# A four-layer graph network on one core: a one-hot matrix in bf16, and three elementwise steps moved from VectorE to ScalarE

## The chip, the cores and the metric

The kernel runs on one core of one Trainium2 chip. The metric is the device time of one launch in microseconds (us). Three launches of the kernel before took 5717.65, 5735.95 and 5736.4 us; the median is 5735.95 us. One more execution, taken with the profiler, took 5731.62 us.

## The reference, cut to what matters

There are 64 graphs of 256 nodes with 128 features, and an adjacency matrix of zeros and ones for each. Four layers follow each other, each with a residual and a layer norm:

```python
# layer 0: the largest relu(p_i + q_j + b) over the neighbours j of i
h = relu(p[:, :, None, :] + q[:, None, :, :] + b) * adj[..., None];  x = LN(x + max(h, axis=2))
# layer 1: three ELU projections, two of them aggregated over the graph
in_rep, out_rep, node_rep = elu(x @ W_in.T + b_in), elu(x @ W_out.T + b_out), elu(x @ W_node.T + b_node)
upd = concat([adj @ in_rep, node_rep, adj.T @ out_rep]);             x = LN(x + tanh(upd @ W_upd.T + b_upd))
# layer 2: two normalised graph convolutions;                        x = LN(x + ...)
# layer 3: for each pair gelu(LN(m_j + m_i + b1)), summed over the neighbours, then a projection and a layer norm
agg = einsum('bijo,bij->bio', gelu(LN(m_j[:, None] + m_i[:, :, None] + b1)), adj); x = LN(x + LN(concat([x, agg]) @ W2 + b2))
```

## The kernel before, in words

For each half h of the neighbours (128 of them), the kernel lays the edges of a graph out in "slots": slot s holds the s-th neighbour of each node that has one. The nodes are sorted by their number of neighbours in that half, so that slot s only needs its first w columns (`RECTS`, 4800 columns in all, `WIDTH`). A matrix of ones and zeros, `hot`, then turns "feature of the s-th neighbour" into a matrix product: layer 0 is a product of `q3` with `hot` and a running maximum (line 665 and the following ones), layer 3 a product of `c3` with `hot`, a normalisation over the features, a Gelu and a running sum.

The sorting is a permutation for each half. `first` (lines 502 to 710) makes it so:

- L509: `nz`, the adjacency in bf16, made on VectorE by comparing `an` (fp32, just loaded) with 1. L511 makes `diff`, which is zero where an entry is 0 or 1.
- L516 and L519: `nz` is transposed by TensorE, and ScalarE copies the result to `aT`.
- L528 to L551: TensorE counts neighbours, ScalarE compares the counts of all nodes (`sign`), which gives each node its place.
- L556 to L561: `perm`, 128 x (2 x 2 x 256), the one-hot of the place, made by four comparisons of `iota_k` (0 to 255 in fp32) with `place`. It is stored in fp32; `as_bf16` reads the upper halves of its words as bf16, with a stride of two.
- L566 and L577: TensorE sorts the columns of `nz` with `perm_b` and transposes `perm_b`; ScalarE copies the results to `nzp` (L571) and `permT` (L581), then makes `rank` (L587) and `lack` (L591), which tells for each slot and node how many neighbours are missing.
- L615: `full`, one where `lack` is zero, on VectorE. SyncE stores it to DRAM (`fulls`, L620), from where layer 3 reads it back in small pieces (`fu`, L763).
- L629 to L641: `hot`, 24 comparisons of `rank` and two more.

`second` is layer 1 (`layer_1`, L215 on). Its node part is the product at L230, the bias at L233 (`nd`, on VectorE), and an ELU: an exponential on ScalarE (L194) and two VectorE instructions (L200, L201). `third` is layer 2 (`layer_2`, L261 on) and the start of layer 3: L810 multiplies `dn` by `perm` in fp32, and four of the ten column tiles of layer 3 (`TODO`, five for each half) are begun (`sums_of`, L718). `last` does the rest of layer 3 (L821 on): a multiplication by the inverse deviation (L839, which waits for its transfer `rs_s`), the Gelu (L841) and the sums (L492).

The program is unrolled over all 64 graphs. In each iteration the four stages run for four different graphs, and `together` mixes their steps by weights (34, 34, 14, 44). What the engines execute is not in this order: a planner at compile time puts an instruction as early as its operands and its buffer allow, where an engine would stand idle by its account. The trace shows it: `nz` is made some 34 us before its first reader, and the three small instructions at L787, L267 and L269 run right after their one buffer comes free, most of an iteration ahead of their use. Each engine works through its own list, and waits at whatever is not ready.

Pools matter in a few places: `work` and `pair` have one buffer of each name (`nz`, `full`, `nd`, `elu_e`), `perm` has three, `permT` four.

Of the kernel before, what the change touches and what calls it, by code (L numbers as in the profile page):

```python
# [9 lines left out]
F32 = mybir.dt.float32  # L10
BF16 = mybir.dt.bfloat16
AF = mybir.ActivationFunctionType
ALU = mybir.AluOpType
# [6 lines left out]
P = 128  # L20
# [23 lines left out]
def kernel(  # L44
# [9 lines left out]
    nc = tc.nc  # L54
    B, N, D = x.shape
    assert N == 2 * P and D == P
    H = N // P
# [8 lines left out]
    nc.vector.memset(half, 0.5)  # L66
    eps_t = consts.tile([P, 1], F32, name="eps_t")
    nc.vector.memset(eps_t, EPS)
    minus1 = consts.tile([P, 1], F32, name="minus1")
    nc.vector.memset(minus1, -1.0)  # L70

# [85 lines left out]
    class Shared:  # L157
# [57 lines left out]
        def layer_1(self, s, an, aT, x1):  # L215

            work, psum, elu = self.work, self.psum, self.elu
            xT = self.to_features(x1, "xT_1", 1)
            yield
            io = work.tile([P, H, 2 * P], F32, name="io")  # L220
            pr = psum()
            for h in range(H):
                nc.tensor.matmul(pr[:, h * N:(h + 1) * N], xT[:, h * P:(h + 1) * P], w1_ioT, start=True, stop=True)
            yield
            for h in range(H):
                nc.vector.tensor_add(io[:, h], pr[:, h * N:(h + 1) * N], b1_io)
            yield from elu(io, io)
            yield
            pn = psum()
            nc.tensor.matmul(pn[:, :N], w1_nodeT, xT, start=True, stop=True)  # L230
            yield
            nd = work.tile([P, N], F32, name="nd")
            nc.vector.tensor_scalar(nd, pn[:, :N], b1_node, None, ALU.add)  # L233
            yield from elu(nd, nd)
            yield
            pg = psum()
            for h in range(H):
                nc.tensor.matmul(pg[:, :N], io[:, h, :P], aT[:, h], start=h == 0, stop=h == H - 1)
            for h in range(H):
                nc.tensor.matmul(pg[:, N:], io[:, h, P:], an[:, h], start=h == 0, stop=h == H - 1)  # L240
            yield
            ag = work.tile([P, 2, N], F32, name="ag")
            nc.scalar.copy(ag, pg.rearrange("p (c n) -> p c n", c=2))
            yield
            pu = psum()
            for h in range(H):
                cols = slice(h * P, (h + 1) * P)
                for c, part in enumerate((ag[:, 0], nd, ag[:, 1])):
                    nc.tensor.matmul(pu[:, cols], part[:, cols], w1_updT[:, c], start=c == 0, stop=c == 2)
            yield  # L250
            y = work.tile([P, H, P], F32, name="y", bufs=2)
            for h in range(H):
                nc.vector.tensor_add(y[:, h], pu[:, h * P:(h + 1) * P], b1_upd)
            nc.scalar.activation(y, y, AF.Tanh)
            yield
            nc.vector.tensor_add(y, y, x1)
            x2 = self.node_tile("x2")
            yield from self.layernorm(x2, y)
            s["x2"] = x2
# [94 lines left out]
    def sparse(ctx):  # L354
# [12 lines left out]
        nc.vector.tensor_copy(ident_b, ident)  # L367
        upto = cs.tile([P, P], BF16, name="upto")
        iota_k = cs.tile([P, N], F32, name="iota_k")
        down = cs.tile([1, N], BF16, name="down")  # L370
        slot1 = cs.tile([P, SLOTS], BF16, name="slot1")
        part1 = cs.tile([P, 1], F32, name="part1")
# [17 lines left out]
        with tc.tile_pool(name="cs_prep", bufs=1) as pp:  # L390
            t = pp.tile([P, P], F32, name="upto_f")
            nc.gpsimd.affine_select(
                out=t, in_=ones, compare_op=ALU.is_ge, fill=0.0, base=0, pattern=[[1, P]], channel_multiplier=-1
            )
            nc.vector.scalar_tensor_tensor(upto, ident, -FAR, t, ALU.mult, ALU.add)
            t = pp.tile([P, N], I32, name="iota_i")
            nc.gpsimd.iota(t, pattern=[[1, N]], base=0, channel_multiplier=0)
            nc.vector.tensor_copy(iota_k, t)
            t = pp.tile([P, 1], I32, name="part_i")
            nc.gpsimd.iota(t, pattern=[[0, 1]], base=0, channel_multiplier=1)  # L400
            part = pp.tile([P, 1], F32, name="part")
            nc.vector.tensor_copy(part, t)
            nc.vector.tensor_scalar(part1, part, 2.0, None, ALU.subtract)
            nc.vector.memset(part1[:3], float(SLOTS))
            nc.vector.tensor_scalar(down, iota_k[:1], -1.0, float(N - 1), ALU.mult, ALU.add)
            nc.vector.tensor_scalar(slot1, iota_k[:, :SLOTS], 1.0 - FAR, None, ALU.add)
            for h in range(H):
                for c in range(H):
                    nc.vector.tensor_scalar(
                        down_c[:, h, c:c + 1], part, -1.0, float(N - 1 - h * P), ALU.mult, ALU.add  # L410
                    )
            for t, slots in ((most, [w for s0, n, w in RECTS for _ in range(n)]), (least, SURE)):
                row = pp.tile([P, N], F32, name="slots")
                nc.vector.memset(row, 0.0)
                for w in slots:
                    if w:
                        nc.vector.tensor_scalar(row[:, :w], row[:, :w], 1.0, None, ALU.add)
                if t is most:
                    nc.vector.tensor_scalar(cover, row[:3], float(SLOTS), None, ALU.subtract)
                for hk in range(H):  # L420
                    pt = ps_mm.tile([P, 512], F32, name="mm")
                    nc.tensor.transpose(pt[:, :P], row[:, hk * P:(hk + 1) * P], ident)
                    for h in range(H):
                        nc.vector.tensor_copy(t[:, h, hk:hk + 1], pt[:, :1])
            t = pp.tile([P, 1], F32, name="gbe")
            nc.scalar.activation(t, be3, AF.Gelu)
            t3 = pp.tile([P, 3], F32, name="gbe3")
            nc.vector.tensor_copy(t3, t.broadcast_to([P, 3]))
            pt = ps_mm.tile([P, 512], F32, name="mm")
            nc.tensor.matmul(pt[:3, :P], t3, w3u[:, 1], start=True, stop=True)  # L430
            rest = pp.tile([3, P], F32, name="u_rest")
            nc.vector.tensor_copy(rest, pt[:3, :P])
            total = pp.tile([3, P], F32, name="u_total")
            nc.vector.memset(total, 0.0)
            for i in range(3):
                t = pp.tile([3, P], BF16, name="u_part")
                nc.vector.tensor_copy(t, rest)
                nc.vector.tensor_sub(rest, rest, t)
                nc.vector.scalar_tensor_tensor(total, t, ident[:3, i:i + 1], total, ALU.mult, ALU.add)
            nc.vector.tensor_scalar(ube, total, -1.0, None, ALU.mult)  # L440
            nc.vector.tensor_scalar(pick, ident[:ROWS, :ROWS], -BIG, None, ALU.mult)
            t = pp.tile([ROWS, g_n, g_w], F32, name="tail_f")
            nc.vector.memset(t, 1.0)
            nc.gpsimd.affine_select(
                out=t, in_=t, compare_op=ALU.is_equal, fill=0.0, base=-row_of(g_s0),
                pattern=[[-1, g_n], [0, g_w]], channel_multiplier=1,
            )
            nc.vector.tensor_copy(tail, t)
            nc.vector.memset(tail[:1, g_n - 1], 1.0)
# [23 lines left out]
        def as_bf16(t):  # L473

            return t.bitcast(BF16).rearrange("... (n two) -> ... n two", two=2)[..., 1]
# [26 lines left out]
        def first(g, s):  # L502
# [3 lines left out]
            an = state.tile([P, H, N], F32, name="an")  # L506
            nc.sync.dma_start(an, adj[ds(g, 1)].rearrange("b (h p) j -> p (b h) j", p=P))
            nz = pair.tile([P, H, N], BF16, name="nz")
            nc.vector.tensor_scalar(nz, an, 1.0, None, ALU.is_equal)  # L509
            diff = pair.tile([P, H, N], BF16, name="diff")  # L510
            nc.vector.scalar_tensor_tensor(diff, an, -1.0, an, ALU.add, ALU.mult)  # L511
            aT = state.tile([P, H, N], F32, name="aT", bufs=3)
# [41 lines left out]
            yield  # L554
            pos = work.tile([P, H, H], F32, name="place")
            nc.vector.tensor_scalar(pos, more, 0.5, 0.5 * (N - 1), ALU.mult, ALU.add)  # L556
            perm = state.tile([P, H, H, N], F32, name="perm", bufs=3)
            for h in range(H):
                for hi in range(H):
                    nc.vector.tensor_scalar(perm[:, h, hi], iota_k, pos[:, h, hi:hi + 1], None, ALU.is_equal)  # L560
            perm_b = as_bf16(perm)  # L561
            yield
            pz = psum()
            for h in range(H):
# [47 lines left out]
            s.update(an=an, aT=aT, perm=perm, permT=permT, lack=lack)  # L612

            full = pair.tile([ROWS, H, N], BF16, name="full")
            nc.vector.tensor_scalar(full, lack, 0.0, None, ALU.is_equal)  # L615
            s["fulls"] = fulls = dram.tile([H, WIDTH], BF16, name="fulls", bufs=5)
            for s0, n, w in RECTS:
                for a, m in ([(s0, n)] if s0 != g_s0 else [(s0, n - 1), (SLOTS - 1, 1)]):
# [163 lines left out]
        def third(g, s):  # L782
# [5 lines left out]

            yield from sh.layer_2(s, s["aT"], deg_of)
            yield  # L790
            x3, perm = s["x3"], s["perm"]

            x3T = sh.to_features(x3, "x3T")
            yield
# [348 lines left out]
```

## Time and profile before

| what | value |
|---|---|
| median of three runs | 5735.95 us (5717.65 to 5736.4) |
| profiled execution: time, span | 5731.62 us, 5729.7 us |
| TensorE matmul (PE) busy | 4529.9 us, 79% |
| VectorE (DVE) busy | 4834.4 us, 84%, 14654 instructions |
| ScalarE (ACT) busy | 4275.2 us, 75%, 6485 instructions |
| of that, loads of activation tables | 1236 x 1283 ns, 1585.8 us |
| the chain that ended last | PE 52%, DVE 29%, ACT 11%, issue 4%, DMA 3% |
| `perm` (L560) | 256 x 347 ns on DVE |
| `nz` (L509), `full` (L615), `nd` (L233) | 64 each, 421, 278 and 476 ns on DVE |

The span is that of all instructions; the time has the launch around it. A busy share is an average over all stages. The "chain that ended last" follows the work back from the last instruction, at each step to what released it, so its shares say which engine's work stood in the way, not how busy an engine was. "Idle before" in a group is the time in which the engine did nothing just ahead of such an instruction, with what ended it.

### The profile page before, as it was taken

To read this page: it belongs to the slowest core of one execution; us is meant where nothing else is said; L and a number is where in the kernel's file an instruction comes from. 1 tells how busy PE (TensorE), PEld (TensorE's weight loads), DVE (VectorE), ACT (ScalarE), POOL (GpSimd) and SP (SyncE) were. 2 spreads that over 40 slices of the span, in tenths; PEclk is the share of its full clock that TensorE was granted. 3 is DMA by queue.
4 is the path that set the end of the run, shared out by engine and by line. 5 is a ranking of instruction groups with operands and counts; after the bars stand their busy time and mean duration, and the time that the engine had idled before them with its cause. 6 is when DMAs were issued, how large, how long until landed. Compare 5 with 4: busy or idle time off the path is not lost.

```text
span 5729.7 us, 83531 instructions
## 1 busy us (share of the span) xinstructions
PE 4529.9 (79%) x27408; PEld 2508.7 (44%) x27408; DVE 4834.4 (84%) x14654; ACT 4275.2 (75%) x6485; POOL 1.9 (0%) x10
## 2 busy tenths in 40 slices
PE   5878878878778778788788788787887887877875
PEld 2444444444444444444444444444444444444443
DVE  6788888888888888888888888888888888888876
ACT  2577777777777777777777777777777777777785
POOL 0000000000000000000000000000000000000000
PEclk8888889889889889888898898898888887888986
DMA  0122222222212221221221222122212212221222
GB/s 22 44 70 63 62 63 72 62 63 66 69 57 70 65 63 63 72 63 62 63 72 62 63 65 70 59 68 65 63 62 72 64 62 63 69 66 60 68 65 74
DMA packets 292813, 365.15 MB, mean 64 GB/s; under 512 B 151952, under 2 KB 210448, under 8 KB 292368
## 3 DMA queue, kind: packets, MB, share of 16 engines
q1 hardware_dynamic: 292368, 359.73, 20.0%
q8 instruction: 217, 3.56, 0.3%
q14 instruction: 228, 1.87, 0.1%
HBM read 345.07 MB, written 14.53 MB: 63 GB/s over the span
## 4 chain that ended last, share of the span: by engine, by line
PE 52%; DVE 29%; ACT 11%; issue 4%; DMA 3%; SPq 0%; DVEq 0%; POOL 0%; ACTq 0%
PE bigp L665 11%; PE bigp L728 8%; DVE pre L839 6%; PE mm L860 5%; DVE lanes L492 4%; PE mm L743 4%; DVE hot L629 4%; DVE pre L732 4%; DVE sums L492 3%; PE bigp L681 3%; DMA rs_s<-scale_line 2%; PE mm L870 2%; PE mm L296 2%; PE mm L699 2%; PE mm L647 2%
## 5 line engine op out<-in xcount | busy, mean ns | idle before, releaser
L665 PE MATMUL bigp<-hot,q 128*128 128x512 fp8e4 (+1 forms) x3840 | 1052.3, 371 | 66.6 <-DVE lanes L492 52.6
L728 PE MATMUL bigp<-hot,c 128*128 128x512 fp8e4 (+1 forms) x3840 | 928.8, 372 | 140.2 <-DVE pre L732 140.2
L732 DVE TENSOR_TENSOR pre<-bigp,dT 128x512 f32<-128x512 f32 (+6 forms) x1664 | 846.3, 530 | 37.8 <-PE bigp L728 33.5
L492 DVE TENSOR_TENSOR lanes<-bigp,lanes 128x512 f32<-128x512 f32 (+6 forms) x1536 | 772.7, 503 | 94.6 <-PE bigp L681 86.9
L839 DVE TENSOR_TENSOR pre<-pre,rs_s 128x1024 f32<-128x1024 f32 (+1 forms) x640 | 732.9, 1150 | 48.6 <-DMA rs_s<-scale_line 48.0
L736 ACT ACTIVATE sq<-pre 128x1024 f32<-128x1024 f32 (+1 forms) x640 | 638.5, 998 | 169.9 <-DVE pre L732 163.9
L841 ACT ACT_TABLE_LOAD x535 | 686.4, 1283 | 9.5
L492 DVE TENSOR_TENSOR sums<-pre,sums 128x1024 f32<-128x1024 f32 (+6 forms) x1024 | 628.8, 614 | 41.2 <-ACT pre L841 40.7
L745 ACT ACTIVATE row<-mm,eps_t 128x256 f32<-128x256 f32 (+1 forms) x640 | 289.6, 453 | 476.9 <-PE mm L743 476.7
L841 ACT ACTIVATE pre<-pre,be,g 128x1024 f32<-128x1024 f32 (+1 forms) x512 | 594.2, 1172 | 57.8 <-DVE pre L839 53.0
L743 PE MATMUL mm<-sq,ones 128*32 128x256 f32 (+1 forms) x5120 | 482.9, 440 | 135.2 <-ACT sq L736 135.2
L74 ACT ACT_TABLE_LOAD x445 | 570.9, 1283 | 7.5
L728 PEld LDWEIGHTS <-c 128*128 128x128 bf16 x3840 | 331.2, 98 | 550.5 <-issue 136.1
L665 PEld LDWEIGHTS <-q 128*128 128x128 bf16 x3840 | 310.8, 97 | 392.6 <-issue 112.0
L296 PE MATMUL mm<-aT,hs 128*128 128x256 f32 x512 | 232.3, 600 | 316.1 <-DVE hs L293 214.8
L629 DVE TENSOR_SCALAR hot<-rank 128x512 fp8e4<-128x512 bf16 (+5 forms) x1536 | 440.5, 348 | 0.0
L681 PEld LDWEIGHTS <-pick 42*128 42x128 bf16 x2944 | 155.8, 95 | 481.5 <-issue 474.2
L296 PEld LDWEIGHTS mm<-aT,hs 128*128 128x128 f32 x512 | 135.6, 293 | 425.8 <-issue 316.1
L860 PE MATMUL mm<-w3u,sums 128*128 128x128 f32 x2048 | 296.7, 289 | 18.4 <-DVE sums L492 16.1
L194 ACT ACT_TABLE_LOAD x221 | 283.5, 1283 | 3.9
L681 PE MATMUL bigp<-lack,pick 42*128 42x36 bf16 (+16 forms) x2944 | 285.7, 187 | 0.0
L860 PEld LDWEIGHTS mm<-w3u,sums 128*128 128x128 f32 x2048 | 254.5, 195 | 37.3 <-issue 17.6
(226 smaller groups left out, 7132.6 us busy)
## 6 DMA issues: line engine op xcount, KB each, us to landing
rs_s<-scale_line SPq DMA_DIRECT2D x512, 512.0 KB
rs_s<-scale_line SPq DMA_DIRECT2D x128, 352.0 KB
an<-in_adj SPq DMA_DIRECT2D x64, 256.0 KB
x<-in_x SPq DMA_DIRECT2D x64, 128.0 KB
line<-row SPq DMA_DIRECT2D x512, 4.0 KB
out<-o SPq DMA_DIRECT2D x64, 128.0 KB
fu<-fulls SPq DMA_DIRECT2D x192, 4.0 KB
vr<-line SPq DMA_DIRECT2D x192, 8.0 KB
```

The lines of the kernel that those rows point to most:

```text
L74: nc.scalar.activation(t, t, AF.Sqrt)
L492: nc.vector.tensor_tensor(lanes[:, :k, :w], src[:, i:i + k], lanes[:, :k, :w], op)
L629: nc.vector.tensor_scalar(hot[:, :, at:at + w], rank[:, :, :w], s0 + i + 1.0 - FAR, None, ALU.is_equal, saturate=False)
L665: nc.tensor.matmul(pt[:, :tl], q3[:, i, h], hot[:, h, t0:t0 + tl], start=i == 0, stop=False)
L681: nc.tensor.matmul(o_, l_, r_, start=False, stop=i == len(todo) - 1)
L728: nc.tensor.matmul(pt[:, :bl], c3[:, k, h], hot[:, h, t0 + b:t0 + b + bl], start=k == 0, stop=k == 2)
L732: nc.vector.tensor_add(block(pre[:, b:], n, w, at), block(pt, n, w, at), widen(dT[:, h, :w], n))
L736: nc.scalar.activation(sq[:, :tl], pre[:, :tl], AF.Square)
L743: nc.tensor.matmul(pr[q * Q:(q + 1) * Q, :tl // 4], ones[:, :Q], v4[:, :, q], start=True, stop=True)
L839: nc.vector.tensor_mul(pre[:, :tl], pre[:, :tl], rs[:, :tl])
L841: nc.scalar.activation(msg[:, :tl], pre[:, :tl], AF.Gelu, bias=be3, scale=g3)
L860: nc.tensor.matmul(pt[:, cols], lanes[:, k, cols], w3u[:, 1], start=k == 0, stop=False)
```

## The change

Four edits:

1. `perm` is bf16 and is compared with a bf16 copy of the iota, `iota_b` (made once). It is read directly as `perm_b`. Since the product at L810 wants fp32, `third` first copies it to an fp32 tile `perm_f` on ScalarE, 128 x 1024, in the pool with one buffer.
2. `nz` is a copy on ScalarE instead of a comparison on VectorE.
3. `full` is relu(1 - lack) on ScalarE instead of a comparison on VectorE. `lack` is a whole number of zero or more, so both give one at zero and zero elsewhere.
4. The bias of `nd` is added on ScalarE, which then also does its exponential.

```diff
+    one_t = consts.tile([P, 1], F32, name="one_t")
+    nc.vector.memset(one_t, 1.0)
...
             nd = work.tile([P, N], F32, name="nd")
-            nc.vector.tensor_scalar(nd, pn[:, :N], b1_node, None, ALU.add)
+            nc.scalar.activation(nd, pn[:, :N], AF.Identity, bias=b1_node)
             yield from elu(nd, nd)
...
+        iota_b = cs.tile([P, N], BF16, name="iota_b")
...
+            nc.vector.tensor_copy(iota_b, t)
...
             nz = pair.tile([P, H, N], BF16, name="nz")
-            nc.vector.tensor_scalar(nz, an, 1.0, None, ALU.is_equal)
+            nc.scalar.copy(nz, an)
...
-            perm = state.tile([P, H, H, N], F32, name="perm", bufs=3)
+            perm = state.tile([P, H, H, N], BF16, name="perm", bufs=3)
             for h in range(H):
                 for hi in range(H):
-                    nc.vector.tensor_scalar(perm[:, h, hi], iota_k, pos[:, h, hi:hi + 1], None, ALU.is_equal)
-            perm_b = as_bf16(perm)
+                    nc.vector.tensor_scalar(perm[:, h, hi], iota_b, pos[:, h, hi:hi + 1], None, ALU.is_equal)
+            perm_b = perm
...
             full = pair.tile([ROWS, H, N], BF16, name="full")
-            nc.vector.tensor_scalar(full, lack, 0.0, None, ALU.is_equal)
+            nc.scalar.activation(full, lack, AF.Relu, bias=one_t[:ROWS], scale=-1.0)
...
-            x3, perm = s["x3"], s["perm"]
+            x3 = s["x3"]
+            perm = work.tile([P, H, H, N], F32, name="perm_f")
+            nc.scalar.copy(perm, s["perm"])
```

## The prediction

> **What bounds the kernel now.** I read the page first. Its engine line and its chain line:
>
> ```profile
> PE 4529.9 (79%) x27408; PEld 2508.7 (44%) x27408; DVE 4834.4 (84%) x14654; ACT 4275.2 (75%) x6485; POOL 1.9 (0%) x10
> PE 52%; DVE 29%; ACT 11%; issue 4%; DMA 3%; SPq 0%; DVEq 0%; POOL 0%; ACTq 0%
> ```
>
> No engine is full, and the chain passes through three of them. So the change, which takes from the busiest (DVE) and gives to the least busy (ACT), must be read stage by stage. The timeline repeats itself every two graphs, 174 us. Busy times of one graph's 87 us, cut where its character changes (graph 24, whose one-hot is made at 2052 us), with the third stretch of its neighbour, graph 25; columns are PE, weight loads, DVE, ACT, POOL, granted clock:
>
> ```profile
> 2000.00:2043.00 43.00, 39.20 (x255) 22.28 (x255) 39.27 (x121) 31.00 (x45) 0.00 (x0) 0.96 0.20 63
> 2043.00:2052.30 9.30, 3.86 (x31) 2.27 (x28) 6.41 (x16) 8.04 (x20) 0.00 (x0) 1.00 0.33 114
> 2052.30:2069.50 17.20, 10.67 (x57) 5.91 (x58) 15.29 (x55) 16.45 (x23) 0.00 (x0) 0.70 0.02 4
> 2069.50:2087.00 17.50, 17.50 (x102) 8.73 (x101) 12.98 (x37) 12.00 (x17) 0.00 (x0) 0.91 0.40 127
> ...
> 2138.80:2158.00 19.20, 10.14 (x57) 5.16 (x58) 16.25 (x56) 16.84 (x23) 0.00 (x0) 0.68 0.09 24
> ```
>
> Stretch 1 belongs to PE and DVE (91% each), stretch 4 to PE (100%). In stretch 3, ACT works 16.45 of 17.2 us while PE waits; with graph 25 it works 16.84 of 19.2. The four edited steps in the groups of instructions (busy us, mean ns, idle before), with rows that price them:
>
> ```profile
> L560 DVE TENSOR_SCALAR perm<-iota_k,place 128x256 f32<-128x256 f32 x256 | 72.7, 347 | 0.1
> L233 DVE TENSOR_SCALAR nd<-mm,b_node 128x256 f32<-128x256 f32 x64 | 30.5, 476 | 5.7 <-PE mm L230 5.6
> L509 DVE TENSOR_SCALAR nz<-an 128x512 bf16<-128x512 f32 x64 | 26.9, 421 | 4.0 <-DMA an<-in_adj 3.6 <-PE mm L566 0.5
> L615 DVE TENSOR_SCALAR full<-lack 42x512 bf16<-42x512 bf16 x64 | 17.8, 278 | 0.0
> L591 ACT ACTIVATE lack<-mm,part 42x512 bf16<-42x512 f32 x64 | 44.2, 691 | 0.0
> L745 ACT ACTIVATE row<-mm,eps_t 128x256 f32<-128x256 f32 x512 | 238.1, 465 | 339.0 <-PE mm L743 338.7
> L736 ACT ACTIVATE sq<-pre 128x1024 f32<-128x1024 f32 x512 | 538.7, 1052 | 167.2 <-DVE pre L732 163.9 <-DVE total_m L688 3.1 <-DVE hs L308 0.2
> ```
>
> Last the ACT timeline of graph 24 around `lack` and around the exponential of `hs` (start, duration):
>
> ```profile
> 2055.50 0.69 ACT L591 ACTIVATE lack<-mm,part 42x512 bf16<-42x512 f32 x1
> 2056.21 1.28 ACT L194 ACT_TABLE_LOAD   x1
> ...
> 2064.87 0.42 ACT L194 ACTIVATE elu_e<-hs 128x256 f32<-128x256 f32 x1
> 2065.31 1.28 ACT L74 ACT_TABLE_LOAD   x1
> 2066.60 0.22 ACT L74 ACTIVATE vr<-vr 108x16 f32<-108x16 f32 x1
> ```
>
> ACT runs without a gap from 2053.6 to 2069. DVE's L200 on that `hs` starts at 2065.78, 0.49 us after the exponential; DVE's L75 on that `vr` at 2066.99, 0.17 us after the root. L75 stands between the two halves of L293, and PE's L296 at 2067.49 waits for those.
>
> [...] L509 (fp32 in) takes 421 ns for 512 elements, L615 (bf16 to bf16) 278, a difference of 143[...]. [...] of 1236 loads none stands at a copy, at L591 or L745. So the change needs no load of its own.
>
> **The change part by part, for one graph.**
>
> *Off DVE.* `nz` 0.42, `full` 0.28, `nd` 0.48, and the four `perm` instructions [...] 347 becomes 280. Together 1.44 us, 92 us over 64 graphs. It is not the gain:
> - `nz` runs at 2008 us. The chain in order of time passes through it for none of the 64 graphs: DVE waits for PE (0.27 us at 2012.1) soon after. I take -0.1; bounds 0 and -0.42.
> - `perm`: PE waits for it 245.5 us in 64 times, but what is late next is ACT. Graph 24: `nzp` (L571) starts at 2053.61 as a Gelu ends, so an earlier L566 gives nothing. Graph 25: ACT waits 0.19 us for L566, so 0.19 is the most.
> - `full` and `nd` stand in a DVE run that the chain follows in half the graphs, but the ACT lag below replaces it.
>
> *On PE*: nothing. The transposes L577 read `perm` with a stride of two and take 217 ns at their shortest, L516 on the contiguous `nz` 219.
>
> *On ACT*[...] the rows above: `nz` 128x512 0.61 (the Abs of `diff`, same size, 0.63), `full` 42x512 with bias 0.69, `nd` 128x256 with bias 0.46, `perm_f` 128x1024 1.05. Less 0.09 overlap each, 2.45 us a graph, 157 us in all: 75% becomes 77%. No DMA is added; SyncE's stores of `full` follow it, and are read back a stage later.
>
> Where they land:
> - `full` becomes ready as `lack` ends. Graph 24: no gap, everything behind is 0.60 later, the exponential of `io` first (2.2 us of slack before DVE wants it), then `row`, `sq`, `agg`, a Gelu, `hs`, `vr`. Graph 25: ACT idles 0.46 after `lack` and gains 0.19 from `perm`, so 0 to 0.05.
> - `nd` in graph 24: L230 ends at 2062.6, a microsecond before the table load for `hs`, so it goes ahead: +0.37. In graph 25 L230 ends at 2154.2, after that load began, and ACT idles 0.46 ahead of the exponential of `nd`: nothing.
> - So in graph 24 `hs` and `vr` come 0.97 later. L75 has 0.17 of slack, so L293 and L296 come 0.80 later (DVE's own relief of about 0.9 is void, since it waits), and stretch 4, where PE is full, begins so much later. With `full` alone it is 0.43. Bounds 0 (both placed behind `vr`) and 0.97.
> - `nz` and `perm_f` (1.47) can go as soon as their buffers are free, after L566 and L810 of the graph before; L810 ends at 2004 us. The small instructions of L787 to L269 do the same, an iteration ahead. That is stretch 1, where ACT idles 12 of 43 us, 3.3 at 2025. Cover is thin in one place: DVE takes the sums at 2009.52, straight after a Gelu ending at 2009.36; a copy ahead of that costs up to 1.05. Bounds 0 and 1.47; I take 0.3, a fifth.
>
> *Sum*: mean of 0.80 and 0.05 is 0.43; +0.30 - 0.10 = 0.63 us a graph. Times 62 (two graphs pass while the pipeline fills): 39 us on the profiled execution's 5731.6, hence 5771. Its median stood 4.3 higher: **5775**, +0.7%.
>
> **Rivals.**
>
> *All hidden.* The planner puts `full` and `nd` into gaps[...] and DVE's relief pays for what is left. For it: 25% of ACT is idle. Against it: not where `lack` is. 5740 (5722 to 5755).
>
> *DVE's relief counts (faster).* One mechanism: `full` and `nd` are planned behind the root of `vr` in stretch 3, so ACT's lag stays under 0.17 us, and then the DVE run is what the chain follows. The chain in order of time has 13.6 us in `nd`, 6.8 in `full`, 17.6 in `perm` (a fifth of it goes, 4), and L566 paced by `perm`, 3 x 67 ns x 63 = 13. That is 37 us: 5699 (5680 to 5715). For it: DVE's 29% of the chain against ACT's 11%. Against it: the 0.02 us between `lack` and its successor.
>
> *The copies fall in the wrong place.* `nz` and `perm_f` land in stretch 2 or 3 or ahead of a Gelu that DVE awaits, at their full 1.47 instead of 0.3: 1.17 x 62 = 73 more, 5848 (5815 to 5880). One more table load of 1.28 us a graph on the path would do as much. For it: the order is planned anew, blind to the real times. Against it: stretch 1 is where their buffers come free.
>
> **How the numbers follow.** Forecast 0.46 (own range 5752 to 5802), all hidden 0.18, DVE's relief 0.20, wrong place 0.16. About 0.5% (29 us) is what a measurement of this kernel can tell from no change: 5707 to 5765. Of the forecast some 0.38 lies above; with the wrong place that is 0.54 slower. The rest of the forecast, all hidden, and a little of the relief make 0.28 the same; 0.18 faster. The range 5700 to 5840 leaves out half of the relief's case and a little over half of the wrong place's.
>
> **What the changed profile would show.** Right: L560 near 280 ns; DVE busy near 4742, ACT near 4450; about 1236 table loads; the third stretch longer in every second graph, with ACT over 95% there and PE's wait at L296 (316 us now, 214.8 for `hs` and 101.3 for `vr`) larger; waits of DVE L75 and L200 on ACT up. Wrong: stretch 3 unchanged or shorter with `full` and `nd` behind `vr`; a changed count of table loads; `perm_f` not in stretch 1; a rhythm other than two graphs.

## The result and the profile after

The changed kernel took 5878.48 us (median of four launches, 5873.3 to 5883.28), the kernel before, beside it, 5729.93 (5717.65 to 5736.4). The ratio is 1.0258, 95% interval 1.0237 to 1.0279: 149 us slower, or 2.4 us a graph over 62 graphs. Slower was the likelier sign of the prediction, but 5775 was some 103 us too low and its range ended at 5840.

The page of the kernel after, its engine line and its chain line (profiled execution 5881.14 us, span 5879.3):

```profile
PE 4570.0 (78%) x27408; PEld 2538.0 (43%) x27408; DVE 4773.1 (81%) x14464; ACT 4473.3 (76%) x6765; POOL 1.9 (0%) x10
PE 53%; DVE 24%; ACT 12%; DMA 6%; issue 3%; SPq 0%; DVEq 0%; POOL 0%; ACTq 0%
```

Every engine's share of the span is lower than before or just above it: the kernel does the same work and waits more. The windows of one graph's stages (graph 24 again; its one-hot is now made at 2099.0 us; columns as before) say where:

```profile
2038.00:2090.00 52.00, 47.77 (x318) 26.97 (x317) 47.35 (x146) 39.82 (x58) 0.00 (x0) 0.98 0.24 70
2090.00:2099.00 9.00, 5.36 (x28) 3.04 (x25) 5.81 (x13) 7.11 (x18) 0.00 (x0) 0.69 0.35 117
2099.00:2123.10 24.10, 13.78 (x63) 7.82 (x64) 16.84 (x57) 18.84 (x28) 0.00 (x0) 0.51 0.15 40
2123.10:2138.00 14.90, 14.88 (x92) 6.92 (x90) 13.17 (x41) 12.46 (x17) 0.00 (x0) 1.00 0.30 86
```

The third stretch is 24.1 us long; before it was 17.2 and 19.2 in turn (cut a little differently). (The first window reaches back beyond one graph, and the last is cut short, so only the middle ones can be set against before.) ScalarE works 18.84 us of it and so is *not* full. TensorE's granted clock there is 0.51, where it was 0.70 and 0.68. Measured alike in both traces, over graphs 6 to 59, from the start of the one-hot to the start of the cast that makes `q` (L501; before L497), the stretch has grown from 20.43 to 23.82 us (+3.4), while the rest of a graph's period has shrunk from 66.81 to 65.94. So the whole loss is here. (The chain line shows DMA at 6% where it was 3%: VectorE waits 69.8 us in all for the transfer `rs_s`, where it waited 48.0. But most of these waits, 62.1 us, lie in the rest of the period, which has shrunk.)

The edited instructions, and what waited, in the groups and the waits of the kernel after (a wait: us in total, times, longest):

```profile
L564 DVE TENSOR_SCALAR perm<-iota_b,place 128x256 bf16<-128x256 bf16 x256 | 55.6, 280 | 0.1
L235 ACT ACTIVATE nd<-mm,b_node 128x256 f32<-128x256 f32 x64 | 30.3, 474 | 68.3 <-PE mm L232 68.3
L513 ACT CAST nz<-an 128x512 bf16<-128x512 f32 x64 | 39.3, 614 | 36.4 <-DMA an<-in_adj 35.9
L619 ACT ACTIVATE full<-lack,one_t 42x512 bf16<-42x512 bf16 x64 | 45.4, 709 | 0.0
L797 ACT CAST perm_f<-perm 128x1024 f32<-128x1024 bf16 x64 | 66.1, 1033 | 1.1 <-DVE perm L564 1.1
```

```profile
PE mm L298 <- DVE hs L295: 465.4, 128, 8.6
ACT nd L235 <- PE mm L232: 68.3, 62, 2.2
```

Their durations are close to those forecast (280, 460, 610, 690 and 1050 ns). New is ScalarE's idle time ahead of `nd`: 68.3 us, 62 times, so in nearly every graph. TensorE's wait for `hs` at L298 (L296 before) is 465 us, against 214.8 for `hs` and 101.3 for `vr` before; that wait alone says little of the loss, for a version below has 405 us and is faster than the kernel before. The timeline of ScalarE in graph 24 shows the two together:

```profile
2113.95 1.07 ACT L740 ACTIVATE sq<-pre 128x1024 f32<-128x1024 f32 x1
2116.22 0.47 ACT L235 ACTIVATE nd<-mm,b_node 128x256 f32<-128x256 f32 x1 [1.21 <-PE mm L232]
2116.71 1.28 ACT L196 ACT_TABLE_LOAD   x1
2118.01 0.42 ACT L196 ACTIVATE elu_e<-hs 128x256 f32<-128x256 f32 x1
2118.33 0.46 ACT L749 ACTIVATE row<-mm,eps_t 128x256 f32<-128x256 f32 x1
2119.30 0.42 ACT L196 ACTIVATE elu_e<-nd 128x256 f32<-128x256 f32 x1 [0.51 <-DVE hs L203]
2121.69 0.37 ACT L301 COPY agg<-mm 128x256 f32<-128x256 f32 x1 [1.98 <-PE mm L298]
```

The square ends at 2115.02. Nothing but list order keeps the load from starting then: in e9 below, where the bias stands behind the exponential of `hs`, it starts 0.02 us after the square. The bias, which belongs to another graph than `hs`, waits 1.21 us for its product, works 0.47, and only then come the load and the exponential of `hs`: 1.69 us late. Earlier in the stretch the mask has its place:

```profile
2102.43 0.69 ACT L595 ACTIVATE lack<-mm,part 42x512 bf16<-42x512 f32 x1
2103.56 0.47 ACT L749 ACTIVATE row<-mm,eps_t 128x256 f32<-128x256 f32 x1 [0.43 <-PE mm L747]
2103.93 0.71 ACT L619 ACTIVATE full<-lack,one_t 42x512 bf16<-42x512 bf16 x1
2104.66 1.28 ACT L200 ACT_TABLE_LOAD   x1
```

It could run as `lack` ends, at 2103.12, while ScalarE waits 0.43 us for `row`'s product. But it stands behind that `row` in the list, and so delays the load by its whole length.

A third thing has changed. Before, two kinds of graph took turns. In one ("A") ScalarE's exponential of `io` followed `lack` at once, and the stretch took 19.24 us on the mean; in the other ("B") it came 6 us later, the exponential at L198 had a table load of its own (32 in all), and the stretch took 21.62. After, all graphs are of kind B: 62 loads at L200, 1260 in all instead of 1236.

### The profile page after: what moved, and what is told of

Read it like the earlier page. It is cut to its first block, busy times and chain, and to the rows that moved or that the text cites. A ratio compares the mean times of both kernels' runs of the same rounds, so it can differ in the third digit from the quotient of the medians.

```text
span 5879.3 us, 83806 instructions
## 1 busy us (share of the span) xinstructions
PE 4570.0 (78%) x27408; PEld 2538.0 (43%) x27408; DVE 4773.1 (81%) x14464; ACT 4473.3 (76%) x6765; POOL 1.9 (0%) x10
## 4 chain that ended last, share of the span: by engine, by line
PE 53%; DVE 24%; ACT 12%; DMA 6%; issue 3%; SPq 0%; DVEq 0%; POOL 0%; ACTq 0%
PE bigp L669 11%; PE bigp L732 9%; DMA rs_s<-scale_line 6%; DVE hot L633 5%; PE mm L866 4%; DVE pre L845 4%; PE mm L747 3%; PE bigp L685 3%; DVE lanes L496 3%; DVE pre L736 2%; DVE sums L496 2%; PE mm L298 2%; PE mm L703 2%; PE mm L876 2%; PE mm L306 2%
## 5 line engine op out<-in xcount | busy, mean ns | idle before, releaser
L736 DVE TENSOR_TENSOR pre<-bigp,dT 128x512 f32<-128x512 f32 (+6 forms) x1664 | 834.2, 531 | 41.4 <-PE bigp L732 40.1
L845 DVE TENSOR_TENSOR pre<-pre,rs_s 128x1024 f32<-128x1024 f32 (+1 forms) x640 | 736.7, 1152 | 71.3 <-DMA rs_s<-scale_line 69.8
L298 PE MATMUL mm<-aT,hs 128*128 128x256 f32 x512 | 251.1, 642 | 465.4 <-DVE hs L295 465.4
L298 PEld LDWEIGHTS mm<-aT,hs 128*128 128x128 f32 x512 | 143.5, 310 | 590.8 <-issue 353.8
L306 PE MATMUL mm<-w,agg 128*128 128x128 f32 x512 | 128.9, 397 | 171.9 <-ACT agg L301 171.9
```

Source lines behind the costliest of these rows:

```text
L736: nc.vector.tensor_add(block(pre[:, b:], n, w, at), block(pt, n, w, at), widen(dT[:, h, :w], n))
L845: nc.vector.tensor_mul(pre[:, :tl], pre[:, :tl], rs[:, :tl])
```

## The experiments

Four theories: **N**, the node bias stands in ScalarE's list ahead of what `hs` needs. **F**, the mask delays ScalarE's list behind `lack`. **R**, the common order B is itself the slower rhythm. **C**, TensorE's granted clock: a small delay puts the products at the stretch's end at half clock (recorded as 0.5), and multiplies itself. Ratios are to the kernel before on the same chip. "Third stretch" is the time from one-hot to `q`, mean of graphs 6 to 59. "Short groups" are those of these 54 graphs in which the last four products L298 start within 1.0 us: at full clock it is about 0.75, at half clock 1.41 to 1.44 (in the kernel before the clock recorded over the group is 1.00 in all 9 short ones, median 0.75 us, and 0.50 in all 45 long ones, median 1.41; in e3 it is 1.00 in all 37 short ones and falls short of it in all 17 long ones). The group behind them (L651, whose result is `q`) is not counted in it. The kernel before, run beside each group of these, took 5722.5 to 5730.7, so times of different groups compare to several us only. Line numbers shift by a few from kernel to kernel: L298 is L296 before and L300 below, the bias's product L232 is L230 and L234.

| kernel | us | ratio, 95% interval | third stretch, rest, us | short groups |
|---|---|---|---|---|
| before | 5730 | 1 | 20.43, 66.81 | 9 |
| after | 5878 | 1.0258 (1.0237 to 1.0279) | 23.82, 65.94 | 11 |
| e1 after, bias on VectorE | 5814 | 1.0157 (1.0140 to 1.0174) | 22.44, 66.28 | 0 |
| e2 after, mask on VectorE | 5817 | 1.0163 (1.0146 to 1.0180) | 22.72, 66.13 | 36 |
| e3 one-hot and `nz` only | 5708 | 0.9976 (0.9964 to 0.9988) | 20.75, 66.08 | 37 |
| e4 bias only | 5826 | 1.0177 (1.0160 to 1.0194) | 18.88, 70.12 | 0 |
| e5 e1 + 14 products | 5771 | 1.0077 (1.0055 to 1.0100) | 21.79, 65.99 | 51 |
| e6 e3 + 14 products | 5679 | 0.9915 (0.9894 to 0.9937) | 20.59, 65.75 | 53 |
| e7 after + 14 products | 5838 | 1.0191 (1.0169 to 1.0213) | 23.28, 65.78 | 13 |
| e8 mask only | 5768 | 1.0079 (1.0054 to 1.0103) | 20.70, 67.10 | 8 |
| e9 after + 6 ahead of L232, bias behind `hs` | 5717 | 0.9989 (0.9981 to 0.9998) | 21.37, 65.84 | 26 |
| e10 e6, node ELU fused | 5672 | 0.9911 (0.9893 to 0.9930) | 20.57, 65.78 | 54 |
| e11 one-hot only | 5744 | 1.0040 (1.0028 to 1.0053) | 20.35, 67.28 | 11 |
| e12 `nz` only | 5747 | 1.0043 (1.0028 to 1.0057) | 20.23, 67.22 | 16 |
| e13 after + 6 behind L232, bias ahead | 5811 | 1.0148 (1.0130 to 1.0165) | 23.17, 65.59 | 29 |
| e14 e9, bias on VectorE | 5795 | 1.0120 (1.0103 to 1.0138) | 22.68, 65.53 | 27 |
| e15 e3 + 6 ahead of L230 | 5705 | 0.9960 (0.9947 to 0.9972) | 21.09, 65.75 | 47 |
| e16 before + 6 ahead of L230 | 5722 | 0.9994 (0.9984 to 1.0004) | 20.20, 66.95 | 26 |

### Which edit costs (e1 to e4, e8)

e1 and e2 each take one edit out of the change; e3 takes out both; e4 and e8 make one alone.

```diff
 # e1: as the change, but
-            nc.scalar.activation(nd, pn[:, :N], AF.Identity, bias=b1_node)
+            nc.vector.tensor_scalar(nd, pn[:, :N], b1_node, None, ALU.add)
 # e2: as the change, but
-            nc.scalar.activation(full, lack, AF.Relu, bias=one_t[:ROWS], scale=-1.0)
+            nc.vector.tensor_scalar(full, lack, 0.0, None, ALU.is_equal)
```

> The changed kernel with the bias of nd back on VectorE, all else as changed. Theory N (the bias stands in ScalarE's list ahead of the table load and the exponential of hs and waits there for TensorE's L232: 1.21 us of idling and 0.47 of work before a load that would otherwise run ahead[...]): 1.7 us a graph at least, with the clock 2.0 to 2.5, so 5735 to 5775. Theory F (full, 0.7 us in a stretch where ScalarE is the bound, is most of it): 5860 or more. Theory R (the new rhythm, in which every graph has the order that every second one had before, is most of it, whichever edit sets it off): 5840 or more. By the compiled order every graph keeps that order in this kernel.

> The changed kernel with full back on VectorE, all else as changed. Theory N: full costs about 0.5 us a graph, so 5840 to 5855. Theory F: 5790 or less. Theory R: 5870 or more.

> The kernel before with nz and perm changed alone, so full and nd stay on VectorE. By the compiled order every graph has the one order, as in the changed kernel. Theory N: 5700 to 5750, the rhythm is harmless. Theory R: 5840 or more. Theory F: 5700 to 5750 too.

> The kernel before with the bias of nd alone on ScalarE. By the compiled order every graph has the other of the two orders here, and the bias stands behind the exponential of hs. Theory N: the edit is harmless in this place, 5700 to 5750. A theory in which the bias costs wherever it stands: 5760 or more, up to 5840.

> The kernel before with full alone on ScalarE; by the compiled order the rhythm of two graphs stays. Theory C: TensorE's products there are at half clock in most graphs already, so full costs only its delay, 0.2 to 0.6 us a graph: 5735 to 5762. The rival, 1.7 us wherever full stands: 5810 or more.

Without both edits the kernel is 0.24% *faster* than before, though all of its graphs are of kind B: R falls. Going from e3, the mask adds 106 us to that (e1 - e3), the bias 108 (e2 - e3), both together 170. Neither alone explains the 149, and e1 and e2 lie in none of the ranges that N, F and R gave for them.

But e3's lists differ from those of e1 and e2 by more than the edit: the planner also moved other work on VectorE and TensorE. The change against e1 is the cleanest view of the bias: over graphs 6 to 59 the three engines run the same instructions in the same order, but for the bias itself. It costs 65 us. The exponential of `hs` starts 18.76 us after the one-hot instead of 17.05 (means), so 1.71 later, about the 1.21 of waiting and the 0.47 of work seen above. That is N. The change against e2 shows the mask nearly as well (the same order on TensorE, and on ScalarE but for the mask; on VectorE some steps of `hot` and `sums` moved too): 62 us. e2 against e3 agrees on N: as many groups L298 are short (36, 37), and yet the stretch is 1.97 us longer. The clock is not out of this, though: the group behind, L651, is short in 6 graphs of e2 and in 34 of e3, and 0.50 of the 1.97 us lies behind the start of L298.

The mask in e1 does something else. TensorE's timeline at the end of graph 24's third stretch, first in e3, then in e1 (start, busy, products):

```profile
2061.50 0.60 PE L230 MATMUL mm<-xT,w_nodeT 128*128 128x256 f32 x2
2062.03 0.64 PE L745 MATMUL mm<-sq,ones 128*32 128x256 f32 x8
2064.75 1.13 PE L296 MATMUL mm<-aT,hs 128*128 128x256 f32 x4 [2.08 <-DVE hs L293]
2065.72 1.03 PE L649 MATMUL mm<-w0qp,xT 128*128 128x256 f32 x4
```

```profile
2094.65 1.06 PE L232 MATMUL mm<-xT,w_nodeT 128*128 128x256 f32 x2
2095.64 1.08 PE L747 MATMUL mm<-sq,ones 128*32 128x256 f32 x8
2097.42 2.08 PE L298 MATMUL mm<-aT,hs 128*128 128x256 f32 x4 [0.70 <-DVE hs L295]
2099.29 1.91 PE L651 MATMUL mm<-w0qp,xT 128*128 128x256 f32 x4
```

The one-hots were made at 2046.3 and 2078.8, so the four products start 18.4 and 18.6 us after them, almost alike. But in e1 each group takes nearly twice as long. In e3 the same two cases stand side by side: graphs with short groups have a stretch of 20.2 us, those with long ones 21.9. In e1 all 54 are long. The mask itself is seen in the exponential of `io`, which starts 0.5 us later in e1 than in e3 (11.99 and 11.46 us after the one-hot, means), with `full` in the same place behind `row` as in the change. So the stretch's 1.7 us (22.44 - 20.75) are 0.5 of delay, as between e1 and the long graphs of e3, and 1.2 for the 37 graphs that turned long. How much of this is the mask and how much the new order of the other work, these two runs don't tell.

e4 lies far above the range that N gave for it (5700 to 5750). It must not be read as the bias's price: its order was made anew, all graphs came out of kind A, its third stretch is the shortest of all (18.88), and it loses its time in the rest (70.12). What costs there was not isolated. e8 keeps the two kinds; its stretch grows by 0.27 us (A from 19.24 to 19.18, B from 21.62 to 22.22) and its rest by 0.29.

### Is it TensorE's clock? (e5, e6, e7)

To e1, e3 and the change, 14 bf16 products a graph are added at the end of the aggregation stretch. They write the unused columns of `pr`, and nobody reads them.

```diff
+            for _ in range(14 if i == 6 else 0):
+                nc.tensor.matmul(pr[:, N:], ident_b, warm_b, start=True, stop=True)
             row = big.tile([P, TILE // 4], F32, name="row")
```

> The changed kernel with nd on VectorE, as in the first run, plus 14 products of 128x256 in bf16 a graph that nothing reads. They write the unused half of a bank that TensorE has at hand, and stand in its list where it waits about 3.5 us for agg, between L298 and L306, so they only keep it busy. Theory C (full's cost of 1.7 us a graph is mostly TensorE's clock: the 0.5 us by which ScalarE is later leaves the products L298, L651 and L306 at the end of the stretch at half clock in all graphs, where without full they ran at full clock in two of three): 5700 to 5750. The rival, that full costs by ScalarE's time alone and the clock is a symptom: 5800 or more, since the work is only added to.

> The kernel with nz and perm changed alone, plus the same 14 products. Theory C: the third of the graphs whose products ran at half clock speeds up by 1.8 us each, 5660 to 5690. The rival: 5705 or more.

> The changed kernel in full, plus the same 14 products. Theory C with the bias of nd still waiting for L232, which is then faster by 0.4 us: 5780 to 5830, that is, most of the 62 us that full adds to nd goes, and some of nd's. The rival: 5870 or more.

Useless work made all three faster, by 43, 29 and 40 us (e5 and e7 by less than C alone had led me to expect). The granted clock of the profiled execution rose with them: from 0.839 to 0.877 (e1, e5), from 0.860 to 0.881 (e3, e6), from 0.840 to 0.866 (the change, e7). In e5 and e7 the three engines' lists over graphs 6 to 59 are those of e1 and the change, apart from the unread products, so C is a cause (in e6 a `row` and some products also changed places). TensorE's timeline in e6, graph 24:

```profile
2041.79 2.66 PE L749 MATMUL mm<-warm_b,ident_b 128*128 128x256 bf16 x12
...
2047.94 1.10 PE L296 MATMUL mm<-aT,hs 128*128 128x256 f32 x4 [2.04 <-ACT elu_e L194]
2048.88 1.03 PE L651 MATMUL mm<-w0qp,xT 128*128 128x256 f32 x4
```

The group starts 3.5 us after the unread products end (2047.94 and 2044.45) and is at the short time, as it is in 53 graphs of 54. In e7 the gain lies elsewhere, for the short groups are hardly more (13 against 11). There it is the bias that waits less:

```profile
ACT nd L235 <- PE mm L232: 19.8, 63, 2.2
```

In the change this was 68.3 us, with the recorded clock at 0.5 from end to end of 54 of the 62 waits; L232's products took 605 ns on the mean, 496 before (L230). With the unread products 48.5 of the 68.3 us are gone. So most of the bias's wait went with the half clock, at which L306 and L232 ran ahead of it: N and C are not separate costs. But C is not all: in e5 51 graphs are short as well, and e5 is still 92 us above e6 (most of what e1 was above e3); and the change with its 14 products is 67 above e5. The half clock at the end of the stretch is not what sets the change apart from the kernel before, either: from the start of the last L298 group to `q` both take the same, 3.48 and 3.46 us, and L298 starts 3.4 us later. It takes away what e3 gains there (2.66).

### Is it the place of the bias? (e9, e13, e14, e16)

In e9 six unread products stand ahead of L232. They make it later by the planner's account too, so that the order written out at compile time puts the bias on ScalarE behind the exponential of `hs`. e13 has the same six products behind L232: the bias stays ahead. e14 is e9 with the bias on VectorE. e16 is the kernel before with the six products.

```diff
 # e9 (in layer_1); e13 has the loop behind the ELU of nd instead
             pn = psum()
+            for _ in range(6):
+                nc.tensor.matmul(pn[:, N:], self.warm[0], self.warm[1], start=True, stop=True)
             nc.tensor.matmul(pn[:, :N], w1_nodeT, xT, start=True, stop=True)
```

> The changed kernel in full, with six unread products of 256 columns set right ahead of L232, so that the order written out puts the node bias on ScalarE behind the exponential of hs and behind the copy of row, still ahead of its own exponential; mask, copies and one-hot stay on ScalarE as in the changed kernel. Theory N (the bias costs because it stands, waiting for L232, ahead of the table load and exponential that hs needs): hs no longer waits for it, the third stretch loses about 1 us, so 5800 to 5830 us, about 50 to 75 under the changed kernel, and TensorE's waits for hs at L298 fall back by some 60 us. If the place of the bias does not matter and its cost is ScalarE's work alone, or the re-made order of the whole graph: 5865 us or more. The six products themselves also keep TensorE busy; a gain that came from this alone would show as more graphs in which the second four-product group of L296 runs at the short time (10 of 54 in the changed kernel), with hs no earlier.

> The changed kernel in full with the same six unread products, set behind L232 instead of ahead of it, between it and L298's products. ScalarE's order is the changed kernel's: the node bias ahead of hs's table load and exponential. If the place of the bias is what costs (N, paid half in the late hs and half in TensorE's clock): 5800 to 5860 us, and hs ready no earlier than in the changed kernel. If the run with the six products ahead of L232 (5717) gained by the products alone: 5715 to 5740 us.

> The run with six unread products ahead of L232, with the node bias back on VectorE (mask, copies and one-hot on ScalarE, or in bf16, as in the changed kernel). N says that behind hs's exponential the bias costs only what 0.47 us of ScalarE costs there, so 5690 to 5725 us, within 30 us of the run with the bias on ScalarE (5717). If the bias costs its 65 to 108 us wherever it stands: 5610 to 5650.

> The kernel before with six unread products ahead of L232 and nothing else. If TensorE's half clock at the end of this stretch costs the kernel before too (45 of its 54 graphs have it): 5660 to 5700 us. If only the changed kernels suffer, since before hides it elsewhere: 5715 to 5740 us.

ScalarE's timeline of e9, graph 24 (one-hot at 2045.2), with the load straight behind the square and the bias (L237) after `row`:

```profile
2060.04 1.07 ACT L745 ACTIVATE sq<-pre 128x1024 f32<-128x1024 f32 x1
2061.13 1.28 ACT L196 ACT_TABLE_LOAD   x1
2062.42 0.42 ACT L196 ACTIVATE elu_e<-hs 128x256 f32<-128x256 f32 x1
2064.64 0.47 ACT L754 ACTIVATE row<-mm,eps_t 128x256 f32<-128x256 f32 x1 [1.80 <-PE mm L752]
2065.02 0.47 ACT L237 ACTIVATE nd<-mm,b_node 128x256 f32<-128x256 f32 x1
```

The exponential of `hs` starts 17.2 us after the one-hot; in the change it was 19.0 (2118.01 - 2099.03). The kernel with all four edits is then at 5717 us, 161 below itself, and 0.11% below the kernel before. That was twice what I expected of it, so e13 asks whether the products did it: with the same six products and as many short groups (29 and 26), but the bias ahead, it is 5811. The other lists agree over graphs 6 to 59. So 94 us go with the place of the bias, 1.64 us of which a graph are seen at the exponential of `hs` (17.11 and 18.75 after the one-hot), and the other 67 (5878 - 5811) go with the products. One thing is left in the 94: the products stand in another place too, and the group L651 is short in all 54 graphs of e9 and in 29 of e13.

In e14 I was wrong: the bias on VectorE should have cost about as much as behind `hs` on ScalarE, and cost 78 us more. VectorE's timeline shows why:

```profile
2083.27 0.61 DVE L312 SCALAR_TENSOR_TENSOR hs<-mm,dinv,b 128x128 f32<-128x128 f32 x2 [1.36 <-PE mm L308]
2085.40 0.48 DVE L237 TENSOR_SCALAR nd<-mm,b_node 128x256 f32<-128x256 f32 x1 [1.53 <-PE mm L234]
2085.80 0.28 DVE L202 TENSOR_SCALAR elu_e<-elu_e 128x256 f32<-128x256 f32 x1
2086.12 0.43 DVE L203 SCALAR_TENSOR_TENSOR hs<-hs,elu_e 128x256 f32<-128x256 f32 x1
```

It is the same fault on the other engine. L237 waits 1.53 us for its product, delayed by the six others, and the ELU of `hs` (L202, L203) stands behind it. In e1 the bias stands there too, but its product is done: VectorE waits 14.5 us in all there, 90.0 in e14. So not the engine of the bias counts, but whether it waits ahead of `hs`.

e16 shows that the six products alone do nothing measurable for the kernel before: they shorten the stretch in graphs of kind B, by 0.5 us (21.62 to 21.09), and leave A as it is.

### The harmless part, the mask again, and a better version (e10, e11, e12, e15)

e11 and e12 make the one-hot's and the adjacency's edit alone, e15 both with the six products. e10 is e6 with the node part's ELU as max(z, 0) + min(exp(z), 1) - 1, z = pn + b:

```diff
+            nc.scalar.activation(e, pn[:, :N], AF.Exp, bias=b1_node)
+            nc.vector.tensor_scalar(nd, pn[:, :N], b1_node, 0.0, ALU.add, ALU.max)
+            yield
+            nc.vector.tensor_scalar(e, e, 1.0, -1.0, ALU.min, ALU.add)
+            nc.vector.tensor_add(nd, nd, e)
```

> The kernel before with the one-hot in bf16 and its FP32 copy on ScalarE alone. Its order keeps the two kinds of graph in turn. If the harmless part's gain (0.25 us a graph for both) comes from the one-hot: 5705 to 5720 us. If it comes from VectorE's relief by the adjacency's copy, or from the one order of all graphs: 5725 to 5740 us, the time of the kernel before.

> The kernel before with the adjacency's bf16 copy on ScalarE alone, in the two kinds of graph in turn. As the prediction priced it (a ScalarE copy of 0.61 us in the first stretch that is hidden or costs up to 0.3 us a graph, VectorE's relief 0.1): 5720 to 5745 us. A gain of 0.25 us a graph, to 5705 to 5715, would say that VectorE's relief counts in the first stretch.

> One-hot and adjacency copy as in the changed kernel, mask and node bias on VectorE, with six unread products ahead of L232. Against the run that has the mask on ScalarE as well, it tells what the mask costs with TensorE kept busy: if its half microsecond of delay counts alone, 30 to 60 us less than that run; if the mask's cost lay in TensorE's clock, 20 us or less. Against the run with fourteen products behind the aggregation (5679) it tells whether six in this place do as well: 5670 to 5690 us.

> The kernel before with the one-hot and the adjacency copy changed, fourteen unread products a graph at the end of the aggregation stretch, and in addition the node part's ELU without a bias step of its own: the exponential reads PSUM with the bias, and VectorE takes max(pn + b, 0) from PSUM and adds. One VectorE pass of 256 columns less a graph and none added on ScalarE. Theory F and N together (the chain hs to L298 and ScalarE's list ahead of hs are what a third stretch is made of, so relief that puts nothing ahead of hs is worth at most its own time): 5640 to 5680 us, the same as or a little under the run with the same products and without the fusion (5679). If the exponential, now waiting for L232 in ScalarE's list where it stood behind the bias before, comes ahead of hs's: 5700 or more.

Each edit alone, in the two kinds of graph in turn, costs 0.40% and 0.43% (21 and 25 us); both together gain 0.24%. So neither edit has the gain in itself. e3 differs from e11 and e12 in its common order B as well: its third stretch is 0.4 to 0.5 us longer, and its rest 1.1 to 1.2 us a graph shorter. e14 is 91 us above e15, whose source differs by the mask alone (its lists on VectorE and TensorE differ in more places, as e3's do from e1's). In both, VectorE's bias waits for L232 ahead of `hs`, 90.0 us with the mask and 64.6 without, and the short groups fall from 47 to 27. So what the mask costs depends on what stands behind it; and e15, with that wait, is no clean base for the mask's price in e9.

e10 and e6 beat both kernels, by 0.89% and 0.85%; they can't be told from each other.

## Why the prediction was wrong

**The third stretch as the place, and ScalarE's list as the cause**: right, and the rest of the period lost nothing. "ACT over 95% there" was wrong: it works 18.84 of 24.10 us, 78%. The list costs by its waits, not by being full. TensorE's wait at L298 grew as forecast, but this proves little: it is 416 us in all in e3 and 482 in e6, and both are faster than the kernel before.

**The durations on ScalarE and VectorE, and nothing on PE**: right (the groups above). The 280 ns of `perm` was the author's estimate; the run shows it, 347 before and 280 after. The 0.09 us of overlap taken off each ScalarE instruction was an estimate too: before, those that start ahead of the end of the one in front overlap it by 0.10 us (median; the table loads left aside); after, `full` and `perm_f` do by 0.10, `nz` by 0.03 and `nd`, which waits, not at all. "Needs no load of its own" was right: none of the 1260 loads stands at an edited line. VectorE's busy time fell by 61 us, not by 92; busy time counts an overlap once, and the sum of its instructions' durations fell by 86.

**"So it goes ahead: +0.37. In graph 25 ... nothing"**: the main failure. The place was seen for graphs of kind A, but only the work was priced, not the wait for L232 in front of it; and kind B was excused by the old order, in which that product came later than the load. The new order put the bias ahead in every graph: 1.21 us of waiting and 0.47 of work in graph 24, 1.71 on the mean (e1 against the change), instead of a forecast mean of 0.19. It cost 65 us with all else in the same order (5878 - 5814), and 94 in another setting (e13 - e9).

**"Graph 25: ACT idles 0.46 after `lack` and gains 0.19 from `perm`, so 0 to 0.05"**: failed. The mask stands behind the `row` that ends that gap, and delays ScalarE there by 0.5 us on the mean (11.99 - 11.46). In e8, which keeps the two kinds, the forecast is the wrong way round: in A the exponential of `hs` is 0.60 us later as forecast, but the stretch is not (forecast +0.43); VectorE's reciprocal of `vr` (L77), whose slack was counted, stands behind `hs` there. In B the stretch is 0.60 longer (forecast 0 to 0.05). In the changed kernel the mask cost 62 us (5878 - 5817).

**The sum left TensorE's clock out.** The lower clock in this stretch was on show (0.70 and 0.68) and was given no term. In the traces of the kernels before and after, the recorded clock is 0.5 or 1.0, nothing between, in 322 and 330 stretches of one value, and all but the last of each trace are a whole multiple of 3.41 us long. A product of L298 (L296 before) takes 634 ns at 0.5 and 379 at 1.0 (medians of those that lie wholly in one value, the same in both traces). e5 to e7 show that adding work pays, by 43, 29 and 40 us. Left out were thus the length of the bias's wait (68.3 us, 19.8 with the unread products) and the 1.2 us a graph by which e1's products at the end are slower than e3's.

**A rhythm of two graphs, assumed to stay**: it did not, as the prediction's last sentence allowed for. By itself it did no harm: e3 has the new order and is 0.24% faster than before. That may be why the "+0.30 for the copies" looks wrong in e3; with the old rhythm the two edits cost 0.35 and 0.40 us a graph (21 and 25 us / 62), where both together were given 0.30 - 0.10.

**The rivals**: "the copies fall in the wrong place" came nearest in time (5848), but for a reason that did not occur: `perm_f` lies in stretch 1, where it was put (52 us after the one-hot), and `nz` at the end of stretch 4 (36 us), not in stretch 2 or 3. So being the nearest was luck. "All hidden" and "VectorE's relief counts" fall: `full` and `nd` went ahead. No run isolates a gain from VectorE's relief.

Adding up along one path: -15 us for e3, +106 for the mask, +65 for the bias: 155, where before and after, run beside each other, differ by 149. The shares depend on the path (the bias first: 108, then 62): both delays meet in the same wait and the same clock, and the first step from e3 also takes in other places of the planner's order. What decides in a given graph between the short and the long group is settled in part: before and after, the recorded clock changes only after whole multiples of 3.41 us, and in e3 the group is short where the rise to 1.0 comes before it (its clock is 1.00 in all 37). Why the rise comes sooner in one graph than in the next, and where e4 loses its time, stays open.

## What to carry to other kernels

An operation moved to another engine's list costs its wait as well as its work (here 1.21 and 0.47 us in graph 24): find what stands behind it there, and ask whether its operand comes later than that work could have started. Where the order is made by a planner, an edit changes the whole order, so a part tried alone (e4) may not show that part's price in the whole, and two runs should be compared list by list before their difference is given to the edit. Where the trace shows a stage's products at half clock, price a delay with what it does to the clock, and try unread products there before moving work about; here they paid in e5 to e7 (43, 29 and 40 us), and not in e16 (0.06%, interval -0.04 to 0.16).

## What was not expected of the hardware

- Fourteen unread products, 2.66 us of TensorE's time for twelve of them in e6, made a kernel of 87 us a graph faster by 0.5 to 0.7%.
- Whether four fp32 products take 0.75 or 1.44 us between their starts differs from graph to graph in one trace with one order: 37 of 54 short in e3, 9 before. In e1, with a mask of 0.7 us on ScalarE and the order made anew, the exponential of `io` came 0.5 us later, and 0 of 54 were short.
- In the traces of the kernels before and after, the clock recorded for TensorE takes two values, 0.5 and 1.0, and changes only after whole multiples of 3.41 us; before, it is 0.5 for 1580 us of the 5673 recorded, after, for 1882 of 5831.
